# A selective-scan kernel: C rows that stay in SBUF, the entry state by ScalarE, seven GpSimd products, earlier convolutions

## The chip, the cores and the metric

The kernel runs on one core of one Trainium2 chip. The core has five engines that run side by side and meet at semaphores: TensorE (PE; its weight loads are listed as PEld), VectorE (DVE), ScalarE (ACT), GpSimd (POOL) and SyncE (SP), which here only issues transfers. Transfers between HBM and SBUF are carried by 16 DMA engines. The metric is device time in microseconds, lower is better. The kernel before takes 11550.38 us, the median of three runs (11546.19 to 11551.36).

## The reference

The input is two images of 96 channels and 128 x 128 pixels. For each image:

```python
x = x + mamba4(ln_c(x))            # four directions: rows, rows reversed, columns, columns reversed
t = tokens(x); t = t + ffn0(ln_t(t)); x = image(t)
x = x + conv3x3(ln_c(x))
t = tokens(x); t = t + ffn1(ln_t(t)); x = image(t)
```

Nearly all time goes to `mamba4`. One direction of it, over L = 16384 tokens, 192 inner channels and 16 states:

```python
xc, z = split(x @ in_w.T)
xc = silu(causal_conv4(xc) + conv_b)
dt_raw, B, C = split(xc @ xproj_w.T)              # 6, 16 and 16 columns
dt = softplus(dt_raw @ dt_w.T + dt_b); A = -exp(A_log)
h[t] = exp(dt[t] * A) * h[t-1] + dt[t] * B[t] * xc[t]   # per channel and state
y[t] = sum over states of h[t] * C[t]
out = ((y + D * xc) * silu(z)) @ outp_w.T
```

B and C of a token are shared by all 192 channels of a direction.

## The kernel before

For each image there are three stages: `normalize` (layer norm, and a row-major and a column-major copy in HBM), `mamba`, and `ffn_and_conv`. The change lies in `mamba`.

`mamba` makes two passes, `pi` = 0 for the forward directions and 1 for the reversed ones. A pass treats two directions together: 2 x 192 channels lie as three groups `g` of 128 partitions. Group 0 is wholly the first direction, group 2 wholly the second, and group 1 holds 64 channels of each. Time is cut into 32 tiles of T = 512 tokens; a (pass, tile) is a *step*, 64 steps for each image and 128 in all. A step has 24 *units* (`nu`, line 385): group by group, pairs of states s = 0, 2, ... 14. Four states make a *quad* and serve two units.

What one unit does:

- SP fetches the B and C rows of a quad from HBM, repeated over all partitions (`row_tile`, L329 to L335). A row tile is 128 x 4 x 512 numbers, 1 MB. B is fetched three quads ahead into four buffers, C two quads ahead into three.
- POOL multiplies the B quad by dt * xc in place (`b_part`, L339), and in every tile but the first of a pass adds the entry state to the first column (L343). The entry state is the decay of the first token (L303, ACT) times the state that the last tile left in `hst` (L342, POOL).
- ACT makes the decays exp(dt * A) of the two states in PSUM (`decay`, L349), two units ahead.
- DVE runs one scan for each state (`scan`, L353). The result goes into the decay's PSUM tile, or into the B buffer for the units of `BY_POOL`.
- `behind` (L435), one unit later, multiplies the states by C, written over the C quad: by DVE (L441), or for the six units of `BY_POOL`, those with s = 0 and s = 8, by POOL (L360), which is issued another unit later. ACT saves the last column in `hst` (L442). PE adds the products into one PSUM bank y with a unit matrix (`sums`, L357): two matmuls, four PE passes, one after the other. The sum of a POOL unit k is issued at unit k + 3 (L454).
- At the first unit of a group, DVE gates the previous group's y with silu(z) (`gated`, L364) before PE may start the next y (L448).

All engines are in program order, which is written out by hand (`in_order`, L150). The main loop (L469 to L490) issues at unit k, in this order: the B fetch of the quad that starts at unit k + 6 and POOL's product for the quad at k + 2 (even k only); what is due at place 0; the first scan of k; `behind(k - 1)`; the decays of k + 2; the second scan; the C fetch of the quad at k + 4 (even k only); what is due at place 1. SP holds its transfers in the same order, and each of them waits until its buffer's last readers are done.

The next step is prepared inside the current one. `prologue` (L214) gives a list `at` of (unit, place, function), L307 to L323: the loads of the input tiles at unit -3; the four-tap convolutions of the three groups as matmuls at units 1, 5 and 9 (`conv`, each into the one PSUM bank `misc`, read out by ACT one unit later); silu at 11; the product that makes the B, C and dt rows at 12 to 14, written to HBM by `rows_to_dram` as `bcd`; dt at 14 to 17; the gate's matmuls at 7, 18 and 21; dt * xc on POOL at 19, 27 and 29. Units from 24 on lie in the step itself. `project` (L367) and `collect` bring a step's result into the image, at units 19 and 27.

In group 1 the channels of the two directions are interleaved, partition 2c for one and 2c + 1 for the other. The weights are permuted for that on the host (`perm`, L605), and for xc and z, whose matmuls write the two directions as two blocks of 64 partitions, `mix` (L253) spreads them with two transfers each. The source of a group-1 row tile is then 64 repeats of a block of two directions:

```python
src = d["bcd"][k, s // 4] if g == 1 else d["bcd"][k, s // 4, g // 2 : g // 2 + 1]
n = src.shape[0]
nc.sync.dma_start(t, src[None].broadcast_to((128 // n, n, 4, T)))
```

Of the kernel before, what the change touches and what calls it, by code (L numbers as in the profile page):

```python
# [10 lines left out]
F32 = mybir.dt.float32  # L11
# [12 lines left out]
T = 512  # L24
# [8 lines left out]
B_AHEAD = 3  # L33
C_AHEAD = 2
AHEAD = 2
BY_POOL = tuple((g, s) for g in range(3) for s in (0, 8))
# [5 lines left out]
def tile_metaformer(ctx: ExitStack, tc: tile.TileContext, a: dict, out: bass.AP):  # L42
# [142 lines left out]
    def mamba(acc, xnr, xnc):  # L185

        with ExitStack() as st:
            pool = lambda n, bufs, **kw: st.enter_context(tc.tile_pool(name=n, bufs=bufs, **kw))

            io, gen, one, mixp, two = (pool(*p) for p in (("io", 2), ("gen", 4), ("one", 1), ("mixp", 1), ("two", 2)))  # L190
# [4 lines left out]
            enter = one.tile([128, NG, S], F32, name="enter")  # L195
# [5 lines left out]
            def inproj(pi, g, w, src, taps):  # L201

                ps = misc()
                for k in taps:
                    se = {"start": k == taps[0], "stop": k == taps[-1]}
                    for d, rows, lo, hi in (
# [4 lines left out]
                        nc.tensor.matmul(ps[rows, :], w(PAIRS[pi][d], k, lo, hi), src[d][:, k : k + T], **se)  # L211
                return ps

            def prologue(pi, i, d):  # L214
# [17 lines left out]
                def conv(g):  # L232
                    d["ps"] = inproj(pi, g, lambda dd, k, lo, hi: inx[:, dd, k, lo:hi], src, (0, 1, 2, 3))

                def conv_out(g):
                    if g == 1:
                        d["xc"] = two.tile([128, NG, T], F32, name="xc")
                    t = mixed("xc") if g == 1 else d["xc"][:, g, :]
                    nc.scalar.activation(t, d["ps"], AF.Identity, bias=convb[:, pi, g : g + 1])  # L239

                def gate(g):
                    d["ps"] = inproj(pi, g, lambda dd, k, lo, hi: inz[:, dd, lo:hi], src, (3,))

                def gate_out(g):
                    if g == 1:
                        d["sz"] = two.tile([128, NG, T], F32, name="sz")
                    nc.scalar.copy(mixed("sz") if g == 1 else d["sz"][:, g, :], d["ps"])  # L247

                def mixed(name):
                    d["mix", name] = mixp.tile([128, T], F32, name="mix")  # L250
                    return d["mix", name]

                def mix(name):  # L253

                    for k in range(2):
                        nc.sync.dma_start(d[name][k:128:2, 1, :], d["mix", name][64 * k : 64 * k + 64, :])
# [44 lines left out]
                def entry(g):  # L301

                    nc.scalar.activation(enter[:, g, :], amat[:, pi, g, :], AF.Exp, scale=d["dt"][:, g, 0:1])  # L303

                first = pi == 0 and i == 0  # L307
                at = [(-3, 1, load), (3, 0, partial(mix, "xc")), (11, 0, partial(silu, "xc"))]
# [360 lines left out]
```

## Time and profile before

| what | value |
|---|---|
| median of three runs | 11550.38 us |
| the profiled execution: its time, its span | 11556.77 us, 11555.0 us |
| the two `mamba` stages, first scan to last | 5069.9 and 5071.1 us |
| busy share of the span: DVE, PE, POOL, ACT | 90%, 90%, 84%, 68% |
| TensorE clock granted | 0.989 of full speed |
| HBM read, written | 3289.04 MB, 54.53 MB |

The profile is one execution with every instruction's start and end. A line of a group names the source line, the engine, the operation, out<-in by the program's names and the shape; then the count, and behind the bar the busy time in us, the mean of one instruction in ns, and the idle time of the engine just before, with what ended it. A line of the waits view says who waited for whom: total us, how often, the longest. A line of the timeline gives the start and the length in us. Names are those of the tiles: `row` is a B or C quad, `da` the decay and the state, `y` the sum, `bcd` the rows in HBM. SPq, POOLq and the like are the engines' instruction queues. Matmuls are pipelined, so the spans of neighbouring ones overlap.

### The profile page before, as it was taken

To read this page: it belongs to the slowest core of one execution; us is meant where nothing else is said; L and a number is where in the kernel's file an instruction comes from. 1 tells how busy PE (TensorE), PEld (TensorE's weight loads), DVE (VectorE), ACT (ScalarE), POOL (GpSimd) and SP (SyncE) were. 2 spreads that over 40 slices of the span, in tenths; PEclk is the share of its full clock that TensorE was granted. 3 is DMA by queue.
4 is the path that set the end of the run, shared out by engine and by line. 5 is a ranking of instruction groups with operands and counts; after the bars stand their busy time and mean duration, and the time that the engine had idled before them with its cause. 6 is when DMAs were issued, how large, how long until landed. Compare 5 with 4: busy or idle time off the path is not lost. (4 is left out here: it accounts for less than half of the span.)

```text
span 11555.0 us, 94102 instructions
## 1 busy us (share of the span) xinstructions
PE 10435.0 (90%) x24208; PEld 3971.4 (34%) x24208; DVE 10421.6 (90%) x10127; ACT 7901.7 (68%) x13564; POOL 9672.3 (84%) x4700
## 2 busy tenths in 40 slices
PE   7999999999999999989989999999999999999899
PEld 2333333333333333333323333333333333333333
DVE  6999999999999999994469999999999999999944
ACT  6767767677677677665567677677676776776655
POOL 5999999999999999991159999999999999999911
PEclk8999999999999999999989999999999999999999
DMA  7888888888888888880068888888888888888800
GB/s 263 335 329 333 333 332 332 330 331 333 329 332 333 330 331 333 329 322 19 26 243 334 328 331 334 330 333 333 333 331 329 332 332 329 331 333 329 319 13 13
DMA packets 540755, 3416.96 MB, mean 296 GB/s; under 512 B 67532, under 2 KB 68652, under 8 KB 143832
## 3 DMA queue, kind: packets, MB, share of 16 engines
q1 hardware_dynamic: 539960, 3410.16, 76.8%
q8 instruction: 196, 3.21, 0.1%
q14 instruction: 343, 2.81, 0.1%
q0 software_dynamic: 256, 0.79, 0.0%
HBM read 3289.04 MB, written 54.53 MB: 289 GB/s over the span
## 5 line engine op out<-in xcount | busy, mean ns | idle before, releaser
L339 POOL TENSOR_TENSOR row<-dtu,row 128x2048 f32<-128x2048 f32 x1536 | 6948.9, 4524 | 283.3 <-DMA row<-bcd 281.6
L357 PE MATMUL y<-row,ident 128*128 128x512 f32 x12288 | 5690.6, 603 | 700.0 <-DVE row L441 699.9
L353 DVE TENSOR_TENSOR_SCAN da<-da,row 128x512 f32<-128x512 f32 x4608 | 5456.9, 1214 | 38.9 <-ACT da L349 5.2
L349 ACT ACTIVATE da<-dt,amat 128x512 f32<-128x512 f32 x6144 | 4246.9, 691 | 170.2
L357 PEld LDWEIGHTS y<-row,ident 128*128 128x128 f32 x12288 | 2256.8, 190 | 4008.4 <-issue 2243.5
L441 DVE TENSOR_TENSOR row<-da,row 128x1024 f32<-128x1024 f32 x2304 | 2776.7, 1205 | 70.2 <-DMA row<-bcd 70.0
L442 ACT COPY hst<-da 128x2 f32<-128x2 f32 x2304 | 368.9, 160 | 2652.2 <-DVE row L441 2649.3
L360 POOL TENSOR_TENSOR row<-row,row 128x1024 f32<-128x1024 f32 x768 | 1807.4, 2353 | 223.0 <-DVE row L353 147.5
L353 DVE TENSOR_TENSOR_SCAN row<-da,row 128x512 f32<-128x512 f32 x1536 | 1852.4, 1206 | 91.9 <-POOL row L339 84.1
L211 PE MATMUL misc<-xa,inx 96*64 96x512 f32 (+1 forms) x2048 | 946.1, 605 | 50.0 <-ACT mix L239 26.8
L211 PE MATMUL misc<-xb,inx 96*64 96x512 f32 (+1 forms) x2048 | 952.3, 608 | 33.6 <-ACT hst L442 24.2
L564 POOL TENSOR_TENSOR acc<-acc,y 96x512 f32<-96x512 f32 x128 | 147.4, 1151 | 991.5 <-DVE y L563 991.5
L298 POOL TENSOR_TENSOR dtu<-dt,xc 128x512 f32<-128x512 f32 x384 | 487.4, 1269 | 106.0 <-DMA xb<-xnc 99.8
L576 PE MATMUL pc<-pad,kw 96*96 96x512 f32 x1152 | 566.4, 593 | 0.0
L211 PEld LDWEIGHTS misc<-xa,inx 96*64 96x64 f32 (+1 forms) x2048 | 327.3, 165 | 581.2 <-issue 438.0
L448 PE MATMUL y<-xc,dmat 128*128 128x512 f32 x768 | 419.5, 628 | 103.6 <-DVE sz L364 103.6
L374 PE MATMUL misc<-sz,gmat 128*96 128x512 f32 x1024 | 484.1, 595 | 0.0
L284 PE MATMUL misc<-rows,dtw 12*128 12x512 f32 x768 | 434.3, 645 | 50.6 <-ACT dt L289 37.9
L364 DVE TENSOR_TENSOR sz<-y,sz 128x512 f32<-128x512 f32 x384 | 264.6, 689 | 229.5 <-PE y L357 198.0
L136 DVE TENSOR_TENSOR xq<-xm,rs 96x512 fp8e5<-96x512 f32 x128 | 87.9, 687 | 392.2 <-ACT rs L132 392.2
L211 PEld LDWEIGHTS misc<-xb,inx 96*64 96x64 f32 (+1 forms) x2048 | 316.5, 164 | 361.9 <-issue 214.1
L372 PE MATMUL misc<-acc,ident 96*96 96x512 f32 x512 | 387.6, 842 | 57.3 <-ACT sz L247 53.8
(76 smaller groups left out, 7449.9 us busy)
## 6 DMA issues: line engine op xcount, KB each, us to landing
row<-bcd SPq DMA_DIRECT2D x3072, 1024.0 KB, 7.4
xc<-mix SPq DMA_DIRECT2D x256, 128.0 KB, 5.4
sz<-mix SPq DMA_DIRECT2D x256, 128.0 KB, 8.9
xa<-xnr SPq DMA_DIRECT2D x124, 193.1 KB, 8.6
xb<-xnc SPq DMA_DIRECT2D x124, 193.1 KB, 8.7
bcd<-rows SPq DMA_DIRECT2D x128, 128.0 KB, 9.5
acc<-in_x_dram SPq DMA_DIRECT2D x16, 768.0 KB, 5.7
xnr<-xn SPq DMA_DIRECT2D x16, 768.0 KB, 4.3
```

What stands on the lines that cost most here:

```text
L211: nc.tensor.matmul(ps[rows, :], w(PAIRS[pi][d], k, lo, hi), src[d][:, k : k + T], **se)
L284: nc.tensor.matmul(d["ps"], w, d["rows"][0 : 2 * RK, :], start=True, stop=True)
L298: nc.gpsimd.tensor_tensor(dtu, d["dt"][:, g, :], d["xc"][:, g, :], ALU.mult)
L339: nc.gpsimd.tensor_tensor(b, d["dtu"][g][:, None, :].broadcast_to((128, 4, T)), b, ALU.mult)
L349: nc.scalar.activation(da[:, j, :], d["dt"][:, g, :], AF.Exp, scale=amat[:, pi, g, s + j : s + j + 1])
L353: nc.vector.tensor_tensor_scan(h[:, j, :], da[:, j, :], b[:, j, :], 0.0, ALU.mult, ALU.add)
L357: nc.tensor.matmul(y, ident, c[:, j, :], start=False, stop=s + j == S - 1)
L360: nc.gpsimd.tensor_tensor(c, h, c, ALU.mult)
L374: nc.tensor.matmul(d["po"], gmat[:, pi, 2 * g - 2 + k, :], d["yg"][g - 1 + k], start=False, stop=k == 1)
L441: nc.vector.tensor_tensor(c, h, c, ALU.mult)
L448: nc.tensor.matmul(y, dmat[:, pi, g, :], d["xc"][:, g, :], start=True, stop=False)
L576: nc.tensor.matmul(pc, kw[:, t, :], rows, start=t == 0, stop=t == 8)
```

## The change

- C: four tiles `crow` of 1 MB stay for the whole stage, one for each quad of states, instead of 12 fetches a step into rotating buffers. `c_fill` refills them. For group 0 all 128 partitions are written; for group 1 partitions 64 to 127 alone get the second direction, for group 2 partitions 0 to 63. It is issued at each even unit k for the tile that units k - 4 and k - 3 used, and for the next group.
- The products by C are written into the B quad, since C must stay. B has five buffers and is fetched four quads ahead; the fetch stands at the end of an even unit, the C fill behind it.
- Entry: the scan starts from 1.0 and the decay's first column is multiplied by `hst` with two one-column activations a unit on ACT. POOL's two entry instructions and ACT's `entry` are gone.
- `BY_POOL` is now s = 2 and s = 8 of each group and s = 4 of group 1: seven units.
- The interleaving of group 1, with `perm` and `mix`, is gone. The source of a group-1 B fetch is now two directions with 64 repeats inside each.
- The prologue's times: loads at -6; convolutions at -3, -1 and 1, each cut into two halves of two taps, at place 0 and place 1; silu at 5; rows at 6 to 8; dt at 8 to 11; gates at 12, 14 and 16; dt * xc at 13, 17 and 21; silu of z at 21.
- The scratch space for software DMA is set to 4096 bytes.

```diff
-B_AHEAD = 3
-C_AHEAD = 2
+B_AHEAD = 4
 AHEAD = 2
-BY_POOL = tuple((g, s) for g in range(3) for s in (0, 8))
+BY_POOL = tuple((g, s) for g in range(3) for s in (2, 8)) + ((1, 4),)
...
-                at = [(-3, 1, load), (3, 0, partial(mix, "xc")), (11, 0, partial(silu, "xc"))]
-                at += [(9, 0, partial(mix, "sz")), (31, 1, partial(silu, "sz"))]
-                at += [(12, 0, rows), (13, 1, rows_out), (14, 0, rows_to_dram)]
-                for g, k in ((1, 1), (0, 5), (2, 9)):
-                    at += [(k, 0, partial(conv, g)), (k + 1, 1, partial(conv_out, g))]
-                for g, k in ((1, 7), (0, 18), (2, 21)):
+                at = [(-6, 1, load), (5, 1, partial(silu, "xc")), (21, 1, partial(silu, "sz"))]
+                at += [(6, 0, rows), (7, 1, rows_out), (8, 0, rows_to_dram)]
+                for g, k in ((1, -3), (0, -1), (2, 1)):
+                    at += [(k, 0, partial(conv, g, (0, 1))), (k, 1, partial(conv, g, (2, 3))), (k + 1, 1, partial(conv_out, g))]
+                for g, k in ((1, 12), (0, 14), (2, 16)):
                     at += [(k, 0, partial(gate, g)), (k + 1, 0, partial(gate_out, g))]
...
+                for g in range(NG):
+                    at += [(8 + g, 0, partial(dt_in, g)), (9 + g, 0, partial(dt_out, g))]
+                at += [(11, 1, partial(softplus, 0, NG))]
+                for g, k in enumerate((13, 24, 26) if first else (13, 17, 21)):
                     at += [(k, 0, partial(dt_u, g))]
...
-                t = gen.tile([128, 4, T], F32, name=f"row{k}", bufs=ahead + 1)
-
-                src = d["bcd"][k, s // 4] if g == 1 else d["bcd"][k, s // 4, g // 2 : g // 2 + 1]
+                t = gen.tile([128, 4, T], F32, name="row", bufs=B_AHEAD + 1)
+                src = d["bcd"][0, s // 4] if g == 1 else d["bcd"][0, s // 4, g // 2 : g // 2 + 1]
                 n = src.shape[0]
-                nc.sync.dma_start(t, src[None].broadcast_to((128 // n, n, 4, T)))
+                nc.sync.dma_start(t, src[:, None].broadcast_to((n, 128 // n, 4, T)))
                 return t
 
-            def b_part(i, d, g, s, b):
+            crow = [one.tile([128, 4, T], F32, name=f"crow{q}") for q in range(S // 4)]
+
+            def c_fill(n, g, q):
+
+                if n < len(steps):
+                    part = (slice(0, 128), slice(64, 128), slice(0, 64))[g]
+                    src = state[n]["bcd"][1, q, int(g > 0)]
+                    nc.sync.dma_start(crow[q][part], src[None].broadcast_to((part.stop - part.start, 4, T)))
+
+            def b_part(d, g, b):
                 nc.gpsimd.tensor_tensor(b, d["dtu"][g][:, None, :].broadcast_to((128, 4, T)), b, ALU.mult)
-                if i > 0:
-                    if s == 0:
-                        nc.gpsimd.tensor_tensor(enter[:, g, :], enter[:, g, :], hst[:, g, :], ALU.mult)
-                    nc.gpsimd.tensor_tensor(b[:, :, 0], b[:, :, 0], enter[:, g, s : s + 4], ALU.add)
 
-            def decay(pi, d, g, s):
+            def decay(pi, i, d, g, s):
...
+                if i > 0:
+                    for j in range(2):
+                        nc.scalar.activation(da[:, j, 0:1], da[:, j, 0:1], AF.Copy, scale=hst[:, g, s + j : s + j + 1])
                 return da
 
-            def scan(j, da, b, h):
-                nc.vector.tensor_tensor_scan(h[:, j, :], da[:, j, :], b[:, j, :], 0.0, ALU.mult, ALU.add)
+            def scan(i, j, da, b, h):
+                nc.vector.tensor_tensor_scan(h[:, j, :], da[:, j, :], b[:, j, :], float(i > 0), ALU.mult, ALU.add)
...
-                h, c = hs.pop(k), cs.pop(k)
+                h, b, c = hs.pop(k), cs.pop(k), crow[s // 4][:, s % 4 : s % 4 + 2, :]
                 if (g, s) not in BY_POOL:
-                    nc.vector.tensor_tensor(c, h, c, ALU.mult)
+                    nc.vector.tensor_tensor(b, h, c, ALU.mult)
...
                 if k % 2 == 0:
-                    fetch(k + 2 * B_AHEAD, 0, B_AHEAD, bs)
                     feed(k + AHEAD)
...
                 if k % 2 == 0:
-                    fetch(k + 2 * C_AHEAD, 1, C_AHEAD, cs)
+                    fetch(k + 2 * B_AHEAD)
+                    if 4 <= k < total + 4:
+                        cn, cu = divmod(k - 4, nu)
+                        cg, cq = cu // 8, cu % 8 // 2
+                        c_fill(cn + (cg == 2), (cg + 1) % 3, cq)
                 issue(k, 1)
...
-        "bcw": grouped(bcw[:, perm]),
-        "dtw": dtw[:, :, perm],
+        "bcw": grouped(bcw),
+        "dtw": dtw,
```

## The prediction, made before the result was known

> **What bounds the kernel now.** I read the page's busy shares first, then the two scan passes as windows, the waits of VectorE, then the waits of the queue that issues the transfers.
>
> ```profile
> PE 10435.0 (90%) x24208; PEld 3971.4 (34%) x24208; DVE 10421.6 (90%) x10127; ACT 7901.7 (68%) x13564; POOL 9672.3 (84%) x4700
> ```
>
> ```profile
> 133.80:5203.70 5069.90, 4600.58 (x10559) 1748.50 (x10560) 4899.04 (x4414) 3561.72 (x6118) 4752.91 (x2274) 1.00 0.85 330
> ...
> 5906.30:10977.40 5071.10, 4602.72 (x10559) 1751.16 (x10560) 4899.57 (x4414) 3561.83 (x6119) 4751.90 (x2274) 1.00 0.86 330
> ```
>
> The columns are length, then busy time of PE, PEld, DVE, ACT and POOL, clock, DMA share, GB/s. A pass has 64 steps: 5069.90/64 = 79.22 us a step, in which DVE is busy for 76.55, POOL 74.3, PE 71.9 and ACT 55.7. DVE is the bound; it waits for 2.67 us a step. Its step holds 48 scans, 18 C products and 3 gatings; with a gating at 0.61 us from start to start, a scan or a product takes (76.55 - 1.83)/66 = 1.13 us.
>
> ```profile
> DVE sz L364 <- PE y L357: 198.0, 207, 3.1
> ...
> DVE row L441 <- DMA row<-bcd: 70.0, 121, 1.3
> ```
>
> ```profile
> SPq L335 <- PE y L357: 6879.4, 1404, 11.1
> ```
>
> These are totals, times and the longest wait. DVE's two waits are small. But the queue that fetches rows stands for 6879/128 = 54 us a step until PE has summed a quad and so freed its buffer. All transfers stand behind that wait, since SP issues in order. One step shows what it costs DVE:
>
> ```profile
> 2525.94 5.31 PE L357 MATMUL y<-row,ident 128*128 128x512 f32 x12
> ```
>
> ```profile
> 2529.57 0.32 SPq L335 DMA_DIRECT2D row<-bcd  x1
> ```
>
> ```profile
> 2535.58 1.23 DVE L441 TENSOR_TENSOR row<-da,row 128x1024 f32<-128x1024 f32 x1 [0.72 <-DMA row<-bcd]
> ```
>
> The middle four of PE's twelve passes are the late sum of unit 0, a GpSimd product; at their end (8 x 0.43 us in) SP issues the C fetch, which lands 5.9 us later, and the product of unit 6 has then stood for 0.72 us. So this loop has no slack already.
>
> ```profile
> DMA packets 540755, 3416.96 MB, mean 296 GB/s; under 512 B 67532, under 2 KB 68652, under 8 KB 143832
> ...
> q1 hardware_dynamic: 539960, 3410.16, 76.8%
> ...
> row<-bcd SPq DMA_DIRECT2D x3072, 1024.0 KB, 7.4
> ```
>
> A quad is 128 packets of 8 KB. Quads queued one behind another land 2.49 us apart (the middle of the trace's landings that follow closely); one alone lands about 4.8 us after its issue: 2.3 fixed and 2.5 of packets on 16 DMA engines.
>
> **The change, part by part.** The sum is made against the profiled execution, 11556.8 us, 6 above the median. Outside the 128 steps lie 11556.8 - 128 x 79.22 = 1417 us, untouched.
>
> Seventh GpSimd product: DVE loses one of 1.13 us. Units with s = 0 are now DVE's, so a product stands between a scan and the gating, and PE has 1.13 us more for y: that wait (198.0/128 = 1.55 us) goes. Without waits a step would take 79.22 - 2.67 - 1.13 = 75.4 us.
>
> The groups by shape give the prices (count, busy us, mean ns):
>
> ```profile
> L339 POOL TENSOR_TENSOR row<-dtu,row 128x2048 f32<-128x2048 f32 x1536 | 6948.9, 4524 | 283.3 <-DMA row<-bcd 281.6 <-ACT da L349 0.3
> ...
> L360 POOL TENSOR_TENSOR row<-row,row 128x1024 f32<-128x1024 f32 x768 | 1807.4, 2353 | 223.0 <-DVE row L353 147.5 <-issue 72.0 <-DMA row<-bcd 0.8
> L298 POOL TENSOR_TENSOR dtu<-dt,xc 128x512 f32<-128x512 f32 x384 | 487.4, 1269 | 106.0 <-DMA xb<-xnc 99.8 <-ACT dt L293 6.2
> ...
> L343 POOL TENSOR_TENSOR row<-row,enter 128x4 f32<-128x4 f32 x1488 | 298.3, 200 | 116.6
> ...
> L303 ACT ACTIVATE enter<-amat,dt 128x16 f32<-128x16 f32 x372 | 109.4, 294 | 0.0
> ```
>
> Entry: POOL loses 12 adds of 0.20 and 3 products of 0.22 and gains one product of 2.35, -0.7 us: 12 x 4.52 + 7 x 2.35 + 3 x 1.27 = 74.6 us, just below 75.4. ACT gains 48 activations of one column and loses 3 of 0.29. Neither end is shown: 0.16 (the two-column copy of L442) to 0.29 (L303, also scaled by a pointer), with 0.03 between: 9 to 15 us, ACT 64 to 70 of 75. I take 0.29, the same kind. Cover: ACT waits 2649/128 = 21 us a step for products. Where it is gone, behind the three clusters of table load, function, table load (1.28 + 1.48 + 1.28 us), the exponentials come up to 0.6 us later: 0 to 1.8 us a step, 0.5 taken. Queued behind are only later exponentials and DVE's scans.
>
> Convolutions: same matmuls, six halves of 1.7 us where three runs of 3.4 stood; the load comes three units earlier and the halves follow it after about 7 us, where such loads land in 8.6. PE may stand there for 2 us, and some 4 us at the rows' product, which follows the silu's cluster at once. PE is idle for 7.3 us a step, which covers both; without cover they delay sums and so fetches. On POOL the three products dt by xc go from units 19, 27 and 29 to 13, 17 and 21, the same work, two of them off the start of the next step. On SP the write of the rows goes from unit 14 to 8, eight units before its first reader, and the B fetch from the head of an even unit to its end, two units further ahead. Per step the SP queue loses four mix transfers (0.55 us of issue each), and C falls from 12 quads to 4 and 8 halves, 20 MB of rows for 24.
>
> Buffer release is the first cost. Products now go into the B quad, so a B fetch waits for PE's sums as only C's did, and each C fill is issued behind a B fetch. GpSimd's units are now s = 2, the second of a quad: the sum comes at unit 4, not 3, and the fetch placed at unit 2 waits for it. Clock: us from a step's first scan, nothing waiting. PE: gating over at 6.3, unit 0's matrix and sums to 9.0, half a convolution to 10.7, ScalarE's copy, projection (3.4) to 15.1, sums of units 2, 3 and 1 (1.75 each) to 20.4. B is issued at 20.5 and C lands at 20.5 + 4.8 + 2.5 = 27.8; the product of unit 6 is due at 23.2: 4.6 us (3.2 if PE has no backlog). Unit 14: due 9.0 after unit 11's product starts; its chain is two sums (5.0 with the first product), 4.8 for B, 1.2 to 2.4 for half a quad: 11.0 to 12.2, so 2.0 to 3.2, 2.6 taken. Unit 22: the same. Unit 2: 1.0 (0 to 1.5). Together 10.8 us.
>
> The shape of group 1's B fetch is the second. Its source was 64 repeats of two directions; now two directions come first, 64 repeats of each inside. No row shows such a source. Cheap end: as the interleaved one, 2.5 us of packets on 16 engines. Dear end: the two outer entries go to one engine each, 64 packets one after the other: 8 x 2.49 = 19.9 us (21.8 at the 24.0 GB/s that 3410 MB in 76.8% of 16 engines make). The nearest row in bytes is the interleaved fetch, but it differs in just this. What the rows share is this: 67,532 small packets stand against some 4,130 issues, sixteen each (the landings), and every outermost count here (128, 96, 64) divides by 16. Shares cut from the outermost dimension explain that; two entries can't be cut so. I take the dear end.
>
> [...]
>
> Dear sum, on those two engines, in order of issue (landing = start + 2.3 + packets). B of unit 8 waits for the last sum of the step before: issued 4.4, lands 26.6; C of units 4 and 5 behind it 29.1, so product 5, due at 19.8, starts then. B of unit 10: 49.0, C of 6 and 7: 51.5 = product 6. B of 12: 71.4, half C of 8 and 9: 72.6 = product 8. B of 14: 92.5, half C of 10 and 11: 93.8 = product 11. From there DVE needs 36.8 to the step's end, and 2.6 twice: 135.8 us. Lower end, the two engines never idle: 4 x 19.9 + 8 x 2.49 + 4 x 2.49 + 8 x 1.24 + 1.5 of loads = 121. Upper, with 21.8: 143.5. The other waits above are shorter and vanish in these. 128 x 135.8 + 1417 = 18,799; less the 6 us to the median, 18,790 (16,905 to 19,785).
>
> **The rivals.** *Sixteen engines after all:* the release waits alone decide: 75.4 + 10.8 + 0.5 = 86.7, 128 x 86.7 + 1417 = 12,510 us (12,000 to 12,920 at the terms' ends). For it: the interleaved fetch, with an outermost count of 64, lands hardly later than the others. Against: that count divides by 16.
>
> *Not slower:* sixteen engines, and the fills land in time because PE frees quads before SP asks: 128 x 75.4 + 1417 = 11,070, where POOL's 74.6 is next. It decides where DVE's waits stay under 79.22 - 75.4 = 3.8 us a step. For it: a sixth fewer bytes. Against: unit 6 already waits with C fetched first and a sum one unit earlier.
>
> *The change not doing what it says:* refilled halves cut row traffic only if a half costs half; if it costs a whole, 10 us more of engine time, inside the dear sum's upper end.
>
> **How the numbers follow.** Dear end 0.85, sixteen engines with waits 0.10, not slower 0.05. The dear case's bounds, 16,905 and 19,785, widened by 1% for loads and packet times, 16,700 to 20,000, hold it 19 times in 20, which is 0.81 of all; the rivals lie outside. A measurement of this kernel tells 0.2% from no change. Faster 0.04 and same 0.01 come from the last case; slower 0.95.
>
> **What would show it.** Right: row fetches of group 1 landing 20 us and more after issue, fewer than 16 small packets for them, DMA share falling to some 0.37 (20 MB at 24 to 26 GB/s on each of 16 engines is 50 us of 136) while DVE waits for rows at products 5, 6, 8 and 11; busy times per step unchanged but for one product. Sixteen engines: landings of 5 to 10 us, waits at units 6, 14 and 22 only. Wrong altogether: DVE busy over 97% in the windows. What I can't price is how two engines alone run: if a packet takes much under 311 ns (the trace's middle for 8 KB), the time falls below the range.

## The result, and the profile after

The changed kernel takes 22,359.32 us (median of 4; 22,353.42 to 22,380.92) where the kernel before took 11,550.87 beside it: a ratio of 1.9361, 95% interval 1.9328 to 1.9395. The forecast had the direction and the main mechanism; its range (16,700 to 20,000) lies below the time.

The page's busy times, and the first of the two scan passes as a window (length, busy time of PE, PEld, DVE, ACT and POOL, clock, DMA share, GB/s), after; the second pass is within 0.3% of it:

```profile
PE 12296.0 (55%) x24208; PEld 4734.0 (21%) x24208; DVE 10414.6 (47%) x9999; ACT 8981.2 (40%) x19138; POOL 9602.9 (43%) x2968
```

```profile
127.10:10597.40 10470.30, 5520.16 (x10539) 2127.32 (x10538) 4896.30 (x4350) 4097.62 (x8904) 4707.48 (x1405) 0.74 0.40 131
```

A step is 10470.30/64 = 163.6 us where it was 79.2. VectorE is busy for 76.5 of it, as before, so the 84 us that came on top are waits. TensorE has the same 24,208 matmuls and is busy for 1,861 us more: its clock fell from 1.00 to 0.74. VectorE's waits (total, times, the longest):

```profile
DVE row L424 <- DMA crow<-bcd: 9449.4, 921, 35.9
...
DVE sz L349 <- PE y L342: 907.0, 254, 6.0
```

Seen unit by unit, the mean wait over 124 steps (all but the first and the last of each image) is 14.6 us ahead of the product of unit 5, 20.3 at unit 6, 16.4 at 8, 16.1 at 11: the four products that the forecast named. The transfers:

```profile
DMA packets 427101, 2812.98 MB, mean 126 GB/s; under 512 B 52172, under 2 KB 53292, under 8 KB 95704
...
q1 hardware_dynamic: 426296, 2806.11, 38.1%
```

The share fell to 38.1% (0.37 was forecast, which is partly luck: the forecast had the engines busy for 50 us of a step of 136, and the trace has 64.9 of 164). While a fetch of group 1 runs, the packet list shows 12 to 13 packets of 8 KB starting in 2 us, of 315 ns each: two engines' worth; elsewhere about 100. One step on SP's queue (start, duration of the issue itself) shows something nobody had counted:

```profile
5046.25 0.47 SPq L312 DMA_DIRECT2D row<-bcd  x1
5046.77 0.59 SPq L322 DMA_DIRECT2D crow<-bcd  x1
5047.92 0.55 SPq L312 DMA_DIRECT2D row<-bcd  x1
...
5065.26 12.80 SPq L312 DMA_DIRECT2D row<-bcd  x1
5078.11 19.55 SPq L322 DMA_DIRECT2D crow<-bcd  x1
...
5110.58 10.85 SPq L266 DMA_DIRECT2D bcd<-rows  x1
```

The step's first scan is at 5032.6. The first slow fetch, the third line, is issued 15.3 us in, not 4.4, with a B and a C quad just ahead of it. Later, with slow fetches in the queue, an issue that takes half a microsecond elsewhere stands for 10 to 20.

### The profile page after: what moved, and what is told of

The parts are those of the page before. It is cut to its first block, busy times and chain, and to the rows that moved or that the text cites. A ratio compares the mean times of both kernels' runs of the same rounds, so it can differ in the third digit from the quotient of the medians.

```text
span 22351.6 us, 95142 instructions
## 1 busy us (share of the span) xinstructions
PE 12296.0 (55%) x24208; PEld 4734.0 (21%) x24208; DVE 10414.6 (47%) x9999; ACT 8981.2 (40%) x19138; POOL 9602.9 (43%) x2968
## 3 DMA queue, kind: packets, MB, share of 16 engines
q1 hardware_dynamic: 426296, 2806.11, 38.1%
## 4 chain that ended last, share of the span: by engine, by line
DMA 53%; PE 33%; DVE 6%; issue 2%; ACT 2%; POOL 2%; SPq 1%; another core or an unknown queue 0%; DVEq 0%; POOLq 0%; ACTq 0%
DMA crow<-bcd 49%; PE y L342 17%; PE misc L211 8%; DMA xa<-xnr 3%; DVE row L424 3%; PE pc L563 2%; DVE da L338 2%; PE misc L359 2%; SPq L312 1%; DVE row L338 1%; PE misc L357 1%; DMA row<-bcd 1%; PE xm L121 1%; PE v L127 1%; POOL row L325 1%
## 5 line engine op out<-in xcount | busy, mean ns | idle before, releaser
L342 PE MATMUL y<-row,ident 128*128 128x512 f32 x12288 | 6974.8, 712 | 6751.8 <-DVE row L424 6611.1
L424 DVE TENSOR_TENSOR row<-da,crow 128x1024 f32<-128x1024 f32 x2176 | 2639.3, 1213 | 9452.8 <-DMA crow<-bcd 9449.4
L338 DVE TENSOR_TENSOR_SCAN da<-da,row 128x512 f32<-128x512 f32 x4352 | 5172.6, 1215 | 368.9 <-POOL row L325 275.1
L345 POOL TENSOR_TENSOR row<-row,crow 128x1024 f32<-128x1024 f32 x896 | 2102.9, 2347 | 7130.7 <-DMA crow<-bcd 4957.5
L342 PEld LDWEIGHTS y<-row,ident 128*128 128x128 f32 x12288 | 2723.7, 230 | 10945.0 <-issue 7622.2
L338 DVE TENSOR_TENSOR_SCAN row<-da,row 128x512 f32<-128x512 f32 x1792 | 2139.9, 1206 | 504.8 <-ACT da L334 498.0
L211 PE MATMUL misc<-xa,inx 96*64 96x512 f32 (+1 forms) x2048 | 1296.4, 781 | 907.0 <-DMA xa<-xnr 705.6
L211 PE MATMUL misc<-xb,inx 96*64 96x512 f32 (+1 forms) x2048 | 1262.9, 763 | 7.7 <-DMA xb<-xnc 4.3
L334 ACT ACTIVATE da<-da,hst 128x1 f32<-128x1 f32 x5952 | 1149.8, 232 | 96.4
L237 ACT ACTIVATE xc<-misc,convb 128x512 f32<-128x512 f32 x384 | 264.0, 687 | 1516.5 <-PE misc L211 1499.3
```

The source lines that it names most:

```text
L211: nc.tensor.matmul(ps[rows, :], w(PAIRS[pi][dd], k, lo, hi), src[dd][:, k : k + T], **se)
L334: nc.scalar.activation(da[:, j, 0:1], da[:, j, 0:1], AF.Copy, scale=hst[:, g, s + j : s + j + 1])
L338: nc.vector.tensor_tensor_scan(h[:, j, :], da[:, j, :], b[:, j, :], float(i > 0), ALU.mult, ALU.add)
L342: nc.tensor.matmul(y, ident, c[:, j, :], start=False, stop=s + j == S - 1)
L345: nc.gpsimd.tensor_tensor(h, h, c, ALU.mult)
L424: nc.vector.tensor_tensor(b, h, c, ALU.mult)
```

## The experiments

In what follows "fill" is a refill of a resident C quad, "fetch" a fetch of a B quad. A "stand" is idle time of an engine just ahead of an instruction. Waits are means per step over the same 124 steps.

**The shape, taken out of the change and put into the kernel before.**

```diff
-                nc.sync.dma_start(t, src[:, None].broadcast_to((n, 128 // n, 4, T)))
+                for h in range(n):
+                    nc.sync.dma_start(t[h * (128 // n) : (h + 1) * (128 // n)], src[h][None].broadcast_to((128 // n, 4, T)))
```

> Kernel after, with one edit: group 1's B quad is fetched by two transfers of 64 partitions, 64 repeats outermost in each, in place of one with two directions outermost. Theory (two DMA engines carry that one transfer): the long waits for C rows at units 5, 6, 8 and 11 (67 us a step together) go, and what is left is the wait for buffers to come free that the prediction's first rival priced: 12,510 us, 12,000 to 12,920; the two halves land within 10 us of issue. Rival (the new order of fetches and fills behind PE's late sums is what costs, not the shape): still over 16,000 us, with waits at the same units.

Measured 14,593.37 us, ratio 1.2634 (1.2615 to 1.2653): 7,766 us below the changed kernel, but 2,080 over the first rival's 12,510. VectorE's wait for C rows, 9,449 us above, is now:

```profile
DVE row L425 <- DMA crow<-bcd: 1652.3, 601, 10.4
```

At units 5 and 11 it is gone, at 6 and 8 it is 6.2 and 0.5 us a step. The other way round, before with the two directions first:

```diff
-                nc.sync.dma_start(t, src[None].broadcast_to((128 // n, n, 4, T)))
+                wide = src[:, None].broadcast_to((n, 128 // n, 4, T)) if k == 0 else src[None].broadcast_to((128 // n, n, 4, T))
+                nc.sync.dma_start(t, wide)
```

> Kernel before, with one edit: the B fetches of group 1, four a step, read two directions outermost with 64 repeats inside; C fetches are left as they are. The rows then land on other partitions than the interleaved channels expect, so this kernel computes something else than the reference; every transfer has the same bytes. Theory (two engines): those two engines have 4 x 20 + 8 x 2.5 + 12 x 2.5 + 1.5 = 131 us of packets a step against 79 before, so at least 128 x 131 + 1417 = 18,200 us, up to 21,500 with waits. Rival (the shape is harmless, the loss lies in the other edits): 11,550 us within 2%.

Measured 21,121.99 us, ratio 1.8293 (1.8257 to 1.833), inside the theory's range. The page of that run:

```profile
DMA packets 533587, 3416.93 MB, mean 162 GB/s; under 512 B 60364, under 2 KB 61484, under 8 KB 136664
```

Small packets fell from 67,532 to 60,364, by 7,168 = 128 steps x 4 quads x 14. Each such fetch has 2 landings where it had 16, and 14 went missing from each of 512 fetches: two engines carry it, as the 12 to 13 packets in 2 us of the changed kernel say too.

**The load three units earlier,** in the changed kernel and with the two transfers.

```diff
-                at = [(-6, 1, load), (5, 1, partial(silu, "xc")), (21, 1, partial(silu, "sz"))]
+                at = [(-9, 1, load), (5, 1, partial(silu, "xc")), (21, 1, partial(silu, "sz"))]
...
-                if u == nu - 7:
+                if u == nu - 10:
```

> Kernel after, with one edit: the next step's input tiles are loaded at unit -9 in place of -6, so that the convolution at -3 finds them. Theory (two engines set most of it, and a late load adds to it: PE stands 7.1 us for the tile, with it the late sums, and with them the first slow fetch): PE's wait for the tile goes, the first slow fetch of a step is issued 7 to 9 us sooner than 15.4 us after the first scan, a step takes 154 to 158 us for 163.7, 21,100 to 21,700 us. Rival (the two engines are the only bound, whatever goes before): 22,360 us within 0.5%.

> Both edits: two half transfers for group 1's B quads and the load at unit -9. Theory: as with the halves alone less the wait of the first convolution for its tile, which without slow transfers should be 0 to 2 us a step: 12,250 to 12,510 us. Rival (the load is late even without slow transfers and holds PE for its 7 us): 700 to 900 us under the kernel with the halves alone.

Measured 21,473.49 us (ratio 1.8598, 1.856 to 1.8635), 886 below the changed kernel, and 13,579.51 us (1.1763, 1.1744 to 1.1783), 1,014 below the run with two transfers. So the stand for the load costs 7 to 8 us a step with the shape or without it. TensorE in the changed kernel, its wait for the tile in all, and one stand just ahead of a step (in brackets, what ended the idle time, as far as the profile can tell):

```profile
PE misc L211 <- DMA xa<-xnr: 705.6, 97, 10.6
```

```profile
5020.24 3.70 PE L342 MATMUL y<-row,ident 128*128 128x512 f32 x8 [1.31 <-DVE row L424]
5030.80 1.08 PE L211 MATMUL misc<-xa,inx 96*64 96x512 f32 x1 [6.86 <-ACT da L334]
```

It stands for 6.86 us at the first half (7.1 in the mean), and the passes after it take 0.86 us from start to start, not 0.43. With the load earlier the first line's wait is 17.4 us in all.

**Each fill ahead of the fetch,** in the last of these.

```diff
                 if k % 2 == 0:
-                    fetch(k + 2 * B_AHEAD)
                     if 4 <= k < total + 4:
                         cn, cu = divmod(k - 4, nu)
                         cg, cq = cu // 8, cu % 8 // 2
                         c_fill(cn + (cg == 2), (cg + 1) % 3, cq)
+                    fetch(k + 2 * B_AHEAD)
```

> The kernel with halves by two transfers and the early load (13,579.51 us), and each C fill issued ahead of the B fetch that it stood behind. Theory (buffer release: the fill is late only because it stands on SP behind a B fetch that waits for the late sum of a GpSimd unit): the product's waits at units 2, 6, 8, 14 and 22, 0.6 + 5.6 + 0.6 + 3.7 + 1.9 = 12.4 us a step, go nearly all; 95.0 - 12.4 = 82.6 us a step, about 12,000 us (11,900 to 12,200). Rival (the fills are late because the transfers themselves take turns on the engines, or since PE is late with everything): 13,400 to 13,600, the product's waits above 8 us a step.

Measured 12,682.01 us (1.099, 1.0973 to 1.1006). VectorE's waits, of the run before this edit and then of the run with it:

```profile
DVE row L425 <- DMA crow<-bcd: 1559.5, 614, 7.7
DVE sz L350 <- PE y L343: 635.8, 284, 4.7
```

```profile
L425 DVE TENSOR_TENSOR row<-da,crow 128x1024 f32<-128x1024 f32 x2176 | 2617.0, 1203 | 4.7 <-DMA crow<-bcd 4.6
```

```profile
DVE sz L350 <- PE y L343: 1040.0, 253, 5.4
```

The waits of the products, 12.4 us a step, are gone (the second fence is a group: busy, mean ns, idle before it), as the release theory says. But the gatings now wait 8.3 us for y: the gain is 898 us, not 1,560, and the time lies between the two expectations. What TensorE does there, in windows of 3.41 us (columns as above):

```profile
2769.38:2772.80 3.42, 1.41 (x4) 0.58 (x4) 2.97 (x4) 3.29 (x8) 3.42 (x2) 1.00 1.00 419
2772.80:2776.21 3.41, 3.41 (x6) 1.35 (x5) 3.41 (x4) 2.66 (x8) 3.41 (x2) 0.50 0.49 204
2776.21:2779.62 3.41, 3.41 (x10) 1.49 (x9) 0.68 (x1) 0.73 (x2) 2.89 (x1) 1.00 0.00 0
```

```profile
2771.74 2.77 PE L211 MATMUL misc<-xa,inx 96*128 96x512 f32 x4 [2.01 <-ACT hst L426]
```

The convolution at unit -1 waits 2.01 us for ScalarE to free its one buffer; TensorE is busy for 1.41 of the 3.42 us, and the next window runs at half clock. In these traces the clock is 1.0 or 0.5, and its changes are whole multiples of 3.41 us apart. In this run the window before a fall had TensorE busy for 0.41 of its length (median; 9 in 10 under 0.53), and the window before a rise for 0.80 at least; but some windows at 0.41 to 0.48 were followed by full clock too.

**The old places.** As the last run, but the load, convolutions and what hangs on them at the units of the kernel before.

```diff
-                at = [(-9, 1, load), (5, 1, partial(silu, "xc")), (21, 1, partial(silu, "sz"))]
-                at += [(6, 0, rows), (7, 1, rows_out), (8, 0, rows_to_dram)]
-                for g, k in ((1, -3), (0, -1), (2, 1)):
-                    at += [(k, 0, partial(conv, g, (0, 1))), (k, 1, partial(conv, g, (2, 3))), (k + 1, 1, partial(conv_out, g))]
+                at = [(-3, 1, load), (11, 0, partial(silu, "xc")), (31, 1, partial(silu, "sz"))]
+                at += [(12, 0, rows), (13, 1, rows_out), (14, 0, rows_to_dram)]
+                for g, k in ((1, 1), (0, 5), (2, 9)):
+                    at += [(k, 0, partial(conv, g, (0, 1, 2, 3))), (k + 1, 1, partial(conv_out, g))]
...
```

> As the run with the fill first, but the load, the convolutions (whole, not in halves), the rows' product, the gates, softplus and the products dt by x stand at the units where the kernel before has them. Theory (the halves at units -3 to 2 delay PE's sums at the start of a step: the gating at unit 1 waits 3.3 us for y and the two later gatings 1.8): these waits fall below 1.5 us in sum, 3 to 5 us a step less than the run with the fill first, which is some 11,400 to 11,650 us, granted clock back to 0.98 or more. Rival (the gating waits for the late sum of unit 20, whatever else PE does): within 130 us of the run with the fill first.

Measured 12,366.62 us (1.0713, 1.0695 to 1.0731), 315 less, between the two expectations. The gating at unit 1 no longer waits, and all three wait 2.1 us instead of 8.3; 3.3 us came back as waits for GpSimd, ScalarE and one fill, and the clock stayed at 0.944, not 0.98.

**TensorE filled.** The run with the fill first, with matmuls of zeros ahead of three stands:

```diff
+            zero = one.tile([128, 128], F32, name="zero")
...
+            def fill(n):
+                for y in ys.values():
+                    for _ in range(n):
+                        nc.tensor.matmul(y[:, 0:128], zero, ident, start=False, stop=False)
...
+                at += [(-1, 0, partial(fill, 4)), (6, 0, partial(fill, 6))]
...
+                    if (g, s) == (1, 4):
+                        later(k + 3, 1, True, fill, 4)
```

> The kernel with the fill first (12,682.01 us; VectorE waits 12.5 us a step, of which 4.9 and 3.4 us at the gatings of units 1 and 9 for y), and 14 matmuls a step of a zero matrix by 128 columns, which add nothing to y, put just ahead of three matmuls for which TensorE stands 2.0 to 2.8 us in that trace (the convolution at unit -1, the rows' product, the late sum of unit 10): about 6 us a step of idle work, nothing else changed. Theory (a stand of 2 us or more halves the granted clock for the 3.4 us after it, and the sums that are late come late by this): clock 0.97 or more, the two waits for y fall from 8.3 to under 4 us a step, 11,950 to 12,250 us. Rival (the low clock is only a sign of standing, and the sums wait for other engines): the added matmuls cost what they take or nothing, 12,650 to 13,400 us.

Measured 12,479.3 us (1.0802, 1.0786 to 1.0818): work added, 203 us saved. The waits for y fell from 8.3 to 5.5 us, time at half clock from 1,667 to 1,155 us in all. The 14 matmuls took 3.6 us a step, not 6, so stands were only partly filled. The rival, that the added matmuls win nothing, is out; the theory's size was too large.

**Entry and seventh product, alone in the kernel before.**

```diff
-                    if s == 0:
-                        nc.gpsimd.tensor_tensor(enter[:, g, :], enter[:, g, :], hst[:, g, :], ALU.mult)
-                    nc.gpsimd.tensor_tensor(b[:, :, 0], b[:, :, 0], enter[:, g, s : s + 4], ALU.add)
...
+                    for j in range(2):
+                        nc.scalar.activation(da[:, j, 0:1], da[:, j, 0:1], AF.Copy, scale=hst[:, g, s + j : s + j + 1])
```

```diff
-BY_POOL = tuple((g, s) for g in range(3) for s in (0, 8))
+BY_POOL = tuple((g, s) for g in range(3) for s in (0, 8)) + ((1, 4),)
```

> The kernel before with one part of the change: the state enters by ScalarE, 48 activations of one column a step in place of GpSimd's 12 adds and 3 products. Theory (as forecast: ScalarE has 21 us a step of waits to hide 48 x 0.23 = 11 us in, and only the exponentials behind the table loads come later): 0 to 0.6 us a step, 11,546 to 11,625 us. Rival (GpSimd, 74.3 of 79.2 us busy, was what VectorE really followed): 0.7 us a step less, 11,440 to 11,500 us.

> The kernel before with the entry by ScalarE and a seventh product by GpSimd, that of unit 10. Theory (VectorE is the bound and loses one product of 1.13 us): 0.8 to 1.2 us a step less than the run with the entry alone, some 11,420 to 11,500 us. Rival (GpSimd, now 74.3 - 0.7 + 2.35 = 76 us busy a step, becomes the bound, and the late sum of unit 10 holds one more C fetch): 1 to 4 us a step more, 11,680 to 12,060 us.

> The kernel before with one part of the change: the product of unit 10 by GpSimd too, seven for six; the state still enters by GpSimd. Theory (VectorE is the bound and loses 1.13 us a step, GpSimd's 74.3 + 2.35 = 76.7 still fit in 78): 0.3 to 1.1 us a step less, 11,400 to 11,510 us. Rival (GpSimd becomes the bound, with its waits for B rows behind it): 0.5 to 3 us a step more, 11,610 to 11,930 us.

Measured: the entry alone 11,940.04 us (1.035, 1.0331 to 1.0368), both 11,914.27 (1.0319, 1.0304 to 1.0334), the seventh product alone 11,569.67 (1.0015, 1.0006 to 1.0025). The first and the last lie in neither range that was expected; the second lies in its rival's, but through the entry's cost: the product there saves 26 us. The entry's first lines of waits:

```profile
DVE sz L354 <- PE y L347: 405.6, 232, 6.2
...
DVE da L343 <- ACT da L339: 119.8, 122, 1.0
DVE row L431 <- DMA row<-bcd: 100.8, 114, 1.8
```

Y was waited for 198.0 us before. Exponentials, sums and fetches are all a little late, together 3.1 us a step; ScalarE, which has 1,149.7 us more to do in a span of 11,941, isn't full. TensorE is at half clock for 2.4 us a step; before, in none of the 124 steps. In the 71 steps that have none here a step takes 81.4 us, 2.2 more than before, and in the other 53 it takes 83.6: most of the 3.1 us came without half clock. The seventh product saves its 1.13 us, and the scan of unit 13 then waits 0.98 us for its exponential (0.14 before) and that of unit 16 for GpSimd 0.36.

**Which units GpSimd takes, and who copies.** Both from the run with the old places (12,366.62): first the units of s = 0 and 8 with unit 10; then s = 2 again, with GpSimd copying its own last columns:

```diff
-BY_POOL = tuple((g, s) for g in range(3) for s in (2, 8)) + ((1, 4),)
+BY_POOL = tuple((g, s) for g in range(3) for s in (0, 8)) + ((1, 4),)
```

```diff
-                nc.scalar.copy(hst[:, g, s : s + 2], h[:, :, T - 1])
+                if (g, s) not in BY_POOL:
+                    nc.scalar.copy(hst[:, g, s : s + 2], h[:, :, T - 1])
...
-            def by_pool(h, c):
+            def by_pool(g, s, h, c):
+                nc.gpsimd.tensor_copy(hst[:, g, s : s + 2], h[:, :, T - 1])
```

> The kernel with the fill first and the load and convolutions at their old places (12,366.62 us), and GpSimd's products those of units with s = 0 and 8 and of unit 10, as before, in place of s = 2 and 8 and unit 10: still seven. Theory (a late sum in the second unit of a quad holds its B quad one unit longer, GpSimd then waits for the next B rows, and VectorE's scans of units 12, 14 and 22 for GpSimd, 4.0 us a step): these waits fall by 2 to 4 us, 11,850 to 12,120 us, less what the gatings give back. Rival (GpSimd is simply full with seven products): 12,300 to 12,430 us.

> The kernel with the fill first and the old places (12,366.62 us), where GpSimd itself copies the last column of its seven units to the state, in place of ScalarE. Since the change GpSimd's product is written over the scan's result and so waits for that copy, 532 us in that trace (4.2 us a step). Theory (this wait makes GpSimd late, and VectorE's scans of units 12 and 14 with it, 3.7 us a step): those waits fall by 1.5 to 3 us, 11,980 to 12,180 us. Rival (GpSimd is full with seven products, and seven copies of 0.2 us come to it): 12,340 to 12,550 us.

Measured 12,460.61 us (1.079, 1.0772 to 1.0808) and 12,373.1 us (1.0702, 1.0684 to 1.072). Both theories fall: the scan of unit 14 waits 2.7 us for GpSimd in all three runs. What they share is seven products by GpSimd: in the two runs that follow, the wait falls from 3.4 us with seven to 0.6 with six, though B rows land no sooner.

**Entry by GpSimd again, then six products again,** so that only residency is left. The edits undo those shown above, in the run with the old places.

> The kernel with the fill first and the old places (12,366.62 us), with the state entering by GpSimd as in the kernel before: ScalarE loses 48 short activations a step, GpSimd gains 3 products and 12 adds. Theory (the entry by ScalarE costs here what it cost in the kernel before, 397 us): 11,920 to 12,050 us. Rival (GpSimd is what VectorE waits for, and gets 3 us a step more): 12,400 to 12,750 us.

> As the run with the entry by GpSimd, and six products by GpSimd, those of s = 0 and 8, as in the kernel before: what is left of the change is the resident C quads with halves refilled, plain rows by two transfers, products written into the B quad, and B four quads ahead. Theory (these cost nothing once each fill is issued ahead of the B fetch): 11,480 to 11,640 us. Rival (the B quad held until its late sum, and the product that waits for ScalarE's copy, still cost 1 to 3 us a step): 11,680 to 11,930 us.

Measured 12,241.31 us (1.0594, 1.0578 to 1.0609): the entry costs 125 us in this company, not 397 (between the two expectations). Then 11,888.23 us (1.0289, 1.0269 to 1.0308): the seventh product with s = 2 costs 353 here, and residency with two transfers 334, as its rival had it. The last run's queue and fetches (KB each, us to landing):

```profile
q1 hardware_dynamic: 441656, 2806.18, 85.4%
...
row<-bcd SPq DMA_DIRECT2D x1024, 1024.0 KB, 10.8
...
crow<-bcd SPq DMA_DIRECT2D x1024, 512.0 KB, 13.9
```

Fewer bytes than before (2,806 MB for 3,410) hold the engines for a greater share, 85.4% for 76.8%, and land later (7.4 before). In one step of that trace nine halves that stand in the queue one behind another land within 19.6 us, 2.45 apart, their packets some 650 ns long; whole quads take 2.49 and 311 ns. A half costs a whole: the third rival's condition.

**Residency with interleaved rows.** The kernel before, with resident quads, products into the B quad and B four ahead, each fill ahead of the fetch; B of group 1 stays one interleaved transfer, halves lie on every second partition.

```diff
...
+                    part, m = ((slice(0, 128), 128), (slice(1, 128, 2), 64), (slice(0, 128, 2), 64))[g]
+                    src = state[n]["bcd"][1, q, int(g > 0)]
+                    nc.sync.dma_start(crow[q][part], src[None].broadcast_to((m, 4, T)))
...
-                    nc.vector.tensor_tensor(c, h, c, ALU.mult)
+                    nc.vector.tensor_tensor(b, h, c, ALU.mult)
```

> The kernel before with one part of the change: the C quads stay and are refilled, products are written into the B quad, B is fetched four quads ahead. Rows, mix transfers, the six products and the entry are those of the kernel before, and B of group 1 comes by one interleaved transfer; a half of a C quad goes to every second partition. In the run with two transfers and the entry by GpSimd (e14) the packets of half quads took some 650 ns for 311, so a half held the engines as long as a whole, 2.4 us. Theory (64 partitions take twice as long for each packet wherever they lie, so that residency saves no engine time, and B's two halves cost 4 x 2.4 us a step there): packets of about 650 ns for the halves again, landings shorter than the 10.8 us of that run, 11,540 to 11,720 us. Rival (only 64 partitions in one block are slow): halves at 310 to 350 ns a packet, DMA share under 0.70, 11,400 to 11,560 us.

> The run with interleaved rows and resident C quads (11,980.62 us), where GpSimd itself copies the last column of its six units to the state. There GpSimd's product, written over the scan's result, waits for ScalarE's copy, 946 us in all, 7.4 us a step; the sum of the unit comes late by that, TensorE stands, its clock is at half for 5.2 us a step, and the gating at unit 17 waits 3.4 us for y. Theory (this wait is what residency costs): the gating's wait falls under 2 us and time at half clock under 1 us a step, 11,560 to 11,750 us. Rival (something else of the resident quads holds it, and six copies of 0.2 us come to a GpSimd that is nearly full): 11,930 to 12,100 us.

Measured 11,980.62 us (1.0366, 1.0352 to 1.038), above both ranges. On the packets the rival was right. Of all 8 KB packets 7% take over 450 ns (49% in the run with blocks, 6% before), and

```profile
q1 hardware_dynamic: 474424, 2873.28, 62.7%
...
crow<-bcd SPq DMA_DIRECT2D x1024, 512.0 KB, 6.1
```

Halves in one block of 64 partitions took some 650 ns a packet, halves on every second partition 309, whole quads 311; why, no run shows. But no time was won: with the engines relieved the kernel is 92 us slower than with the blocks. GpSimd's own copies, by the edit above, gave 12,022.91 us (1.0397, 1.0374 to 1.042): the theory of the copy falls a second time. What went with the steps' length in both runs was the clock: steps with less than 1 us at half clock take 80.6 us, the longest 85.2, correlation 0.99. One of the first run's steps with half clock, in windows, and the matmul that stands in the first of them:

```profile
2742.27:2745.68 3.41, 1.80 (x5) 0.76 (x5) 3.41 (x4) 1.92 (x4) 3.41 (x2) 1.00 0.89 283
2745.68:2749.09 3.41, 3.41 (x5) 0.85 (x4) 3.41 (x4) 2.19 (x5) 3.33 (x4) 0.50 0.86 320
2749.09:2752.51 3.42, 3.42 (x5) 1.17 (x4) 3.42 (x4) 2.28 (x5) 3.42 (x1) 0.50 0.05 19
2752.51:2755.92 3.41, 3.41 (x5) 1.35 (x4) 1.32 (x2) 0.69 (x1) 1.12 (x2) 0.50 0.00 0
```

```profile
2743.48 1.12 PE L283 MATMUL misc<-rows,dtw 12*128 12x512 f32 x2 [1.21 <-ACT rows L271]
```

```profile
2759.64 0.69 DVE L371 TENSOR_TENSOR sz<-y,sz 128x512 f32<-128x512 f32 x1 [5.81 <-PE y L364]
```

TensorE stands 1.21 us for ScalarE and 0.40 a little later, is busy for 0.53 of that window, and pays with three windows at half clock; 14 us on, the gating waits 5.81 us for y. So five matmuls of zeros, as long as the stand, were put there:

```diff
                 at += [(12, 0, rows), (13, 1, rows_out), (14, 0, rows_to_dram)]
+                at += [(14, 0, partial(fill, 5))]
```

> The run with interleaved rows and resident C quads (11,980.62 us), and five matmuls a step of a zero matrix by 128 columns, which add nothing to y, put ahead of the first product for dt. There TensorE stands 1.2 us for ScalarE's copy of the rows, 0.4 us more soon after, and its clock is at half over the next units, 5.2 us a step; steps with no half clock take 80.6 us, those with the most 85.2. The five take about 1.2 us, the stand's own length. Theory (that stand takes TensorE under the edge at which the clock is halved, and the gating at unit 17 waits for the sums that come late by it): half clock under 1 us in nearly every step, 80.3 to 80.8 us a step, 11,680 to 11,770 us. Rival (the half clock only goes with something else that is late): 11,950 us or more.

Measured 11,709.65 us (1.0135, 1.0117 to 1.0153): 271 us less, for work added. Not one of the 124 steps has half clock, and all take 80.5 to 80.6 us. In that trace the five stand where the idle time was:

```profile
2672.70 1.28 PE L201 MATMUL y<-ident,zero 128*128 128x128 f32 x10
2674.07 1.12 PE L291 MATMUL misc<-rows,dtw 12*128 12x512 f32 x2
```

The 1.35 us left to the kernel before are about what one wait grew by: the scan of unit 13 stands 1.48 us for its exponential, where it stood 0.14; why that is late was not tested. No version here beats the kernel before.

The way from the changed kernel back, in us, each part undone on top of those above it:

| undone | time | saved |
|---|---|---|
| (the changed kernel) | 22,359 | |
| two directions outermost | 14,593 | 7,766 |
| load only six units ahead | 13,580 | 1,014 |
| fill behind the fetch | 12,682 | 898 |
| halves at the new places | 12,367 | 315 |
| entry by ScalarE | 12,241 | 125 |
| seventh product, s = 2 | 11,888 | 353 |
| resident quads, plain rows | 11,554 | 334 |

## Why the prediction was right and wrong

**Shape: the mechanism right, its price too low.** Two engines, 315 ns a packet, waits at products 5, 6, 8 and 11. It is 72% of the loss (7,766 of 10,808); by the forecast's own two sums it was 18,790 - 12,510 = 6,280.

**The step that failed** is "PE is idle for 7.3 us a step, which covers both", with the convolutions and the load at nothing. The load's stand was put at 2 us and is 7.1 in the mean; with the load earlier (21,473) the first slow fetch goes out at 8.3 us where it was 15.4 (medians), and the step is 7.1 us shorter. The idle time was no cover: what the forecast had for the case "without cover", delayed sums and so fetches, is what happened, and the passes just behind the stand ran at half clock (0.86 us from start to start, not 0.43).

That alone leaves the time above the range. The trace tells where the rest of the dear sum was short. In one step of 166.0 us its points lie so: product 5 at 46.2 for 29.1, then 23.5, 23.1 and 24.9 us to the next for 22.4, 21.1 and 21.2, and 48.3 to the end for 42.0. Of the first 17.1 us, 10.9 are the late issue, most of it the load's stand: B of unit 8 goes out at 15.3, not 4.4. The other 6.2 are what it meets: the B and C quads ahead of it land at 18.2 and 20.7, and it lands at 43.6, where 15.3 + 2.3 + 19.9 make 37.5. The sum had the two engines free for it and its packets at 311 ns throughout. They take some 630 ns at 20.7 to 22 us, while a C quad runs on the other engines, and 313 when the fetch is alone. So the three later fetches take 20.6, 21.8 and 23.3 us for 19.9 (medians over the steps). At the end the products of units 14 and 22 wait 3.6 and 2.4 us (2.6 each was forecast), but the scan of unit 14 also waits 2.1 us for GpSimd and the gating at unit 17 1.7 us for y. What half clock (0.74 in the window) has in all this no run took apart from that kernel, and it is open, too, what SP's held issues cost there.

**Halves at 1.24 us: right on the two engines, wrong elsewhere.** In the queue of the slow fetches the halves take 1.7 and 1.2 us. With 16 engines, a block of 64 partitions took 2.45. The third rival priced it right, as 10 us of engine time, and gave it no chance of its own.

**Buffer release: right.** 10.8 us a step forecast at units 2, 6, 14 and 22; 11.7 measured there once the shape was gone (0.6, 5.6, 3.7, 1.9), and gone when the fill went first. It paid only 7.0 us of that: the waits for y grew from 5.0 to 8.3 us and those of the scans from 1.4 to 4.0.

**Entry: its busy time right, its cost not.** 0.23 us each lies inside the bounds (0.16 to 0.29), but 0.5 us on the path was 3.1 in the kernel before and 1.0 in the variant with the old places. In the kernel before VectorE then waits longer for exponentials, sums and fetches, and 0.9 of the 3.1 us go with the steps at half clock. How one leads to the other is my reading of the waits.

**Seventh product and the wait for y: wrong.** -1.13 and -1.55 us were booked; alone the product gave +0.1, as waits for ScalarE's exponentials (0.8 us) and GpSimd (0.4) took its place, and in the change and most of its variants the waits for y grew. In the kernel before three engines are busy for 76.6, 74.3 and 71.9 us of a step, and ScalarE, at 55.7, is just in time at unit 13; there a saving on one engine is not yet a saving.

**Sixteen engines at 12,510: too low.** The form of it ran at 14,593; 1,014 of the difference is the load's stand and 315 the new places; the remaining 754 no run took apart, and the sum reckoned at full clock where this run has 24.8 us a step at half.

## What to carry to other kernels

Before an idle engine is taken as cover, ask what standing does to it: in the changed kernel's trace, over the same steps, all 481 windows of 3.41 us at full clock in which TensorE was busy for under 0.40 were followed by one at half clock, and so were 76 of 204 with 0.40 to 0.55. In the run with interleaved rows 1.6 us of stands in one window went with steps up to 4.6 us longer, and a few matmuls of zeros put into the stand paid. Look at the outermost count and at the block of partitions of every reshaped transfer: two entries outermost meant two engines (2 landings where there were 16), and 64 adjacent partitions took as long as 128 (2.45 us for 2.49). When the engines are this close to balance, test parts one by one; their prices change with their company.

## What the hardware showed that was not expected

- The kernel before has no half-clock window in its 124 steps, with stands of 1.4 us; 1.2 + 0.4 us in one window of its variant had three. The edge isn't sharp by the busy share: one window of 0.52 in the kernel before was followed by full clock, and with the entry alone windows of 0.53 by either.
- An issue on SP takes 0.5 us, and 12.80, 19.55 and 10.85 when fetches on two engines were waiting in the queue: not only the transfers stand then but the queue's own engine.
- In the step taken apart above, packets of a fetch on two engines took 313 ns alone and some 630 while a quad ran on the other engines.
- Packets of 8 KB into 64 adjacent partitions took 650 ns, into every second partition 309, into 128 partitions 311. Two transfers to blocks of 64 take 2.45 us each in place of 2.49 for one to all 128, but in place of one fetch on two engines they saved 7,766 us.
